# Start of a fused graph kernel: table and node constants move from VectorE to GpSimd, a shared PSUM tile, and a new order of rounds 0 to 3

## Chip, cores and metric

The kernel runs on one core of one Trainium2 chip. The metric is the device time of one execution in microseconds, as the median of several runs; less is better.

## What is computed

Two graph layers act on x, 3327 nodes of 64 features, with an adjacency matrix adj of 3327 x 3327 (about 0.5% ones). The part that costs time is all pairs of nodes (i, j): about 11 million of them.

```python
h = relu(layernorm(x))
# layer 0
x_t  = logmap0(h, c)                       # one scale per node
att  = sigmoid(left[:, None] + right[None, :] + b) * adj     # left = x_t @ w[:D], right = x_t @ w[D:]
x_local = logmap(h[:, None], h[None], c)   # per pair: a scale from dot products, times vectors of i and j
support = einsum('ij,ijd->id', att, x_local)
x = x + proj(expmap(h, support, c), c)
# layer 1
h = relu(layernorm(x)); s = h @ weight
rank = cumsum(adj != 0, axis=1)            # the last 100 neighbours get weights 0.5 ** (how many follow)
x = x + w @ s + bias
```

## The kernel before

**Tiling.** The nodes are padded to 26 blocks of 128. The pairs are cut into strips of target nodes i (8, 8, 6 and 4 blocks wide: `STRIPS`, L29), and each strip runs over all source blocks j from 25 down to 0. One *round* is one tile of 128 x up to 1024 pairs; in strip 0 a round is one block j, so round n handles j = 25 - n. There are 91 rounds.

**One round n**, by helper (lines of the kernel before):
- `load` (L613): SyncE's queue brings the adjacency tile `ad`; five buffers.
- `edges` (L620): VectorE makes the 0/1 `mask`. `count` (L625): TensorE adds the mask into the running count `pc` in PSUM. `read` (L638): the count is read out to `behind`; `ON_ACT` (L35) says on which engine, in strip 0 in turn VectorE (even rounds) and ScalarE (odd rounds).
- `products` (L668): TensorE multiplies the tables `ju` and `jz` (features of block j) with `iu`, `iz` (features of the strip) into a PSUM tile `pq`; there are two of these, used in turn. Two Gelus on ScalarE (L1211, L1212) turn `pq` into the pair's scale.
- `sigmoids` (L651): ScalarE's tanh of left + right into `sg`. `pair_one` (L658): VectorE, sg = (sg + 1) * ad. `pair_two` (L663): VectorE, sg = (pq + WD) * sg.
- `total` (L676): TensorE, `hw`-transposed times sg, summed over j in the PSUM tile `po`. `hw` is a summing table: 64 scaled features and one column for each node.

A strip's sum is then turned and finished per node (`post`, L978), in part on GpSimd; last come the second layer's products (L1252 on).

**The order of work** is written out by hand for TensorE, VectorE and ScalarE (`manual_schedule`, L692): each of the three runs its instructions in the order in which the program states them, and a wait holds up all that follows on that engine. GpSimd and SyncE are ordered by the scheduler. The loop at L1194 starts with round 1; in round n it also counts and reads round n + 1 and makes the mask of round n + 2.

**The start.** Ahead of the loop the features are normalised and scaled. Blocks 24-25 (`last_j`), 0-7 (`first_i`) and 16-23 (`high`) become tables before the loop: `features`, a cast, a subtraction (each feature is kept as two fp16 parts), transposes by TensorE (`turned_to`, L786), copies out of PSUM (`kept`, L794: VectorE `ju`, ScalarE `jz`), and `logits` (L855), which gives `left` and `right` of those blocks. Blocks 8-15 (`low`) are scaled at L896-899 and turned in `last_of_ahead` (L901), which the loop resumes once in each of rounds 1, 2 and 3 (L1238). There VectorE also makes `hw` (L907-911 and L915) and eleven small constants (L917-927). `left_to_dram` (L594) writes `left` out for the later strips. In PSUM `po` has one buffer, shared in turn by logits, `first_left`, the low blocks' transposes, `left_to_dram` and the strip's sum.

GpSimd starts with seven small loads (L460, L471-472), sets constants, and issues six copies of tables (L846).

Of the kernel before, what the change touches and what calls it, by code (L numbers as in the profile page):

```python
# [11 lines left out]
F32 = mybir.dt.float32  # L12
# [10 lines left out]
P = 128  # L23
# [9 lines left out]
AHEAD, LOADS = 1, 4  # L33
SGB, ADB = 5, 5
# [411 lines left out]
def fast(ctx, tc, x, adj_t, r, w_att, b_att, weight, bias, out, flag):  # L446
# [18 lines left out]
    bias_b = across(bias, D, "bias_b")  # L465

# [3 lines left out]
    for half in (slice(0, D), slice(D, P)):  # L470
        nc.gpsimd.dma_start(w_lr[half], bass.AP(tensor=w_att.tensor, offset=w_att.offset, ap=[[1, D], [D, 2]]))  # L471
        nc.gpsimd.dma_start(w2[half], weight)
# [121 lines left out]
    def left_to_dram():  # L594
        plt = ps.tile([P, P], F32, name="po")
# [42 lines left out]
    def read(n, j):  # L638
# [5 lines left out]
        if i * num // den != (i + 1) * num // den:  # L644
# [199 lines left out]
    for to, of in ((jz[:D], iz[D:]), (jz[D:], iz[:D]), (ju[:D], iu[:D]), (ju[D : D + 3], iu[D + 3 : D + 6]),  # L844
                   (ju[D + 3 : D + 6], iu[D : D + 3]), (ju[KB : KB + 7], iu[D:])):
        nc.gpsimd.dma_start(to[:, first_i], of)  # L846

# [7 lines left out]
    def logits(bs):  # L855

        plr = ps.tile([P, NB, 2], F32, name="po")
# [14 lines left out]
    for j in js(0):  # L872
        read(0, j)
    products(0)
    pl = first_left()
    turned_to(p3, high, 0)
    edges(1)
    pq = pq_of[0]
    A.activation(pq, pq, AF.Gelu, scale=-WG / QS)
    A.activation(pq, pq, AF.Gelu, scale=WH)  # L880
# [3 lines left out]
    pair_one(0)  # L884
    for j in js(1):
        count(1, j)
    products(1)
    edges(2)
    A.copy(left_b[:, : strips[0].F], pl[:, : strips[0].F])
    strips[0].left = left_b  # L890
    sigmoids(1)
    for j in js(1):
        read(1, j)
    pair_two(0)
    logits((high,))
    features(low)  # L896
    A.copy(nz[:, low, 0], zf[:, low])
    V.tensor_copy(nu[:, low, :D], zf[:, low])
    V.tensor_sub(nz[:, low, 1], zf[:, low], nz[:, low, 0])

    def last_of_ahead():  # L901

        p4 = ps.tile([P, 16, P], F16, name="po")
        turned_to(p4, low, 0)
        kept(p4, low, 0)
        wn, opx = small("wn"), small("opx")
        V.tensor_scalar(wn, nrm, WA / 2, None, op0=ALU.mult)  # L907
        V.tensor_scalar(opx, x2, c_c, 1.0, op0=ALU.mult, op1=ALU.add)
        V.tensor_mul(hw[:, :, D], opx, wn)
        V.tensor_mul(wn, wn, y)  # L910
        V.tensor_mul(hw[:, 13:, :D], rl[:, 13:], wide(wn[:, 13:], 13))
        logits((low,))
        left_to_dram()
        yield
        V.tensor_mul(hw[:, :13, :D], rl[:, :13], wide(wn[:, :13], 13))  # L915
        yield
        V.tensor_scalar(w2s, w2, 2.0**27 / HS, None, op0=ALU.mult)  # L917
        V.tensor_scalar(ih, babs, 2 / WA, None, op0=ALU.mult)
# [461 lines left out]
```

## Time and profile before

| what | value |
|---|---|
| median of 3 runs | 418.63 us (418.58 to 420.04) |
| the profiled execution | 419.95 us, of which 418.2 us are the span of the trace |
| VectorE (DVE) busy | 377.5 us, 90% of the span |
| ScalarE (ACT) busy | 362.8 us, 87% |
| TensorE (PE) busy | 359.9 us, 86% |
| GpSimd (POOL) busy | 113.4 us, 27%; idle from 27.7 us to 145 us but for one small copy |
| granted TensorE clock, mean | 0.973 |
| round 4's pair_one starts at | 53.42 us |
| a round pair of strip 0, later on | 6.87 us |

The page names source lines (L661 is line 661) and tiles: `sg<-sg,ad` is pair_one, `sg<-pq,sg` pair_two, `mask<-ad` edges, `behind_hi<-pc` a read. Busy shares are means over stages with different limits, so this case has to be read from the timeline between 20 and 60 us. There a start is in us from the span's beginning, then comes the duration, and in brackets the idle time before the instruction and what ended it. Instructions of one engine overlap by some 0.08 us, so the distance of starts is a better measure of cost than the duration.

### The profile page before, as it was taken

The page shows a single profiled execution, that of the slowest core. Times are in us where ns is not written, and L with a number is a line of the kernel's source. Part 1 is how long each engine was busy: PE and PEld are TensorE (multiplying, and loading weights), DVE is VectorE, ACT ScalarE, POOL GpSimd, SP SyncE. Part 2 cuts the span into 40 slices and gives each one's busy share as a digit, 9 for nine tenths or more (in the row PEclk, how much of TensorE's full clock was granted, in tenths as well). Part 3 has the DMA queues.
Part 4 walks back from the last instruction along what each step waited for, and adds up shares of the span by engine and source line. Part 5 has one row for each costly group of instructions (what it writes and reads, how often), then busy time and mean ns, then how long its engine had stood idle before and what let it go on. Part 6 is the DMA issues. An engine that isn't in the chain of part 4 may idle for free. (4 is left out here: it accounts for less than half of the span.)

```text
span 418.2 us, 4717 instructions
## 1 busy us (share of the span) xinstructions
PE 359.9 (86%) x1460; PEld 154.2 (37%) x1460; DVE 377.5 (90%) x559; ACT 362.8 (87%) x409; POOL 113.4 (27%) x224
## 2 busy tenths in 40 slices
PE   0094999999998899999999899999877999898792
PEld 0062333333333333333333444444332333344362
DVE  4989999999999999999999998899989899898841
ACT  3577889999999999999999999999896999787810
POOL 7020000000000073950250063801405183442400
PEclk9999799999999999999999999999898999999987
DMA  7313634444547445444535455444633420000012
GB/s 180 160 40 102 191 100 153 150 153 150 155 146 233 138 127 175 141 121 143 147 116 159 113 152 146 123 146 127 186 116 103 113 88 0 2 0 1 2 25 65
DMA packets 23298, 48.99 MB, mean 117 GB/s; under 512 B 8789, under 2 KB 9245, under 8 KB 23265
## 3 DMA queue, kind: packets, MB, share of 16 engines
q1 hardware_dynamic: 20993, 47.66, 37.9%
q0 software_dynamic: 464, 0.49, 0.7%
q10 hardware_dynamic: 1808, 0.46, 0.6%
q8 instruction: 13, 0.21, 0.2%
q14 instruction: 20, 0.16, 0.1%
HBM read 46.40 MB, written 0.87 MB: 113 GB/s over the span
## 5 line engine op out<-in xcount | busy, mean ns | idle before, releaser
L683 PE MATMUL po<-sg,hw 128*65 128x512 f32 (+1 forms) x364 | 162.2, 570 | 0.4 <-DVE st L958 0.4
L666 DVE SCALAR_TENSOR_TENSOR sg<-pq,sg 128x1024 f32<-128x1024 f32 (+1 forms) x91 | 103.5, 1137 | 7.4 <-ACT pq L1212 6.8
L661 DVE SCALAR_TENSOR_TENSOR sg<-sg,ad 128x1024 f32<-128x1024 f32 (+1 forms) x91 | 103.8, 1140 | 0.1
L656 ACT ACTIVATE sg<-left_b,right 128x1024 f32<-128x1024 f32 (+2 forms) x103 | 99.5, 978 | 0.0
L1211 ACT ACTIVATE pq<-pq 128x1024 f32<-128x1024 f32 (+1 forms) x90 | 86.1, 957 | 2.7 <-PE pq L674 2.5
L1212 ACT ACTIVATE pq<-pq 128x1024 f32<-128x1024 f32 (+1 forms) x90 | 85.2, 946 | 2.9
L683 PEld LDWEIGHTS po<-sg,hw 128*65 128x65 f32 x364 | 49.7, 139 | 70.8 <-issue 56.9
L634 PE MATMUL pc<-mask,ca 128*128 128x512 bf16 (+1 forms) x175 | 64.3, 368 | 12.4 <-DVE behind_hi L649 3.8
L673 PE MATMUL pq<-iu,ju 71*128 71x512 f16 (+1 forms) x182 | 67.8, 373 | 1.5 <-ACT jz L797 1.0
L635 PE MATMUL pc<-mask,cb 128*128 128x512 bf16 (+1 forms) x182 | 65.5, 370 | 1.8 <-ACT behind_lo L645 1.7
L674 PE MATMUL pq<-iz,jz 128*128 128x512 f16 (+1 forms) x182 | 66.3, 371 | 0.0
L623 DVE TENSOR_SCALAR mask<-ad 128x1024 bf16<-128x1024 f32 (+1 forms) x91 | 58.7, 645 | 0.0
L1280 PE MATMUL pw<-wt,s 128*128 128x512 bf16 (+1 forms) x154 | 34.2, 376 | 4.2 <-DVE s L1135 2.2
L635 PEld LDWEIGHTS <-cb 128*128 128x128 bf16 x182 | 17.9, 98 | 53.2 <-issue 41.5
L1030 POOL TENSOR_TENSOR dots<-dots,ih 128x8 f32<-128x8 f32 (+1 forms) x3 | 2.2, 720 | 129.0 <-DVE dots L1050 129.0
L634 PEld LDWEIGHTS <-ca 128*128 128x128 bf16 x175 | 17.3, 99 | 29.6 <-issue 17.7
L1280 PEld LDWEIGHTS <-s 128*128 128x128 f16 x182 | 18.0, 101 | 23.8 <-issue 4.3
L673 PEld LDWEIGHTS <-ju 71*128 71x128 f16 x182 | 18.0, 99 | 22.8 <-DVE sg L666 4.3
L674 PEld LDWEIGHTS <-jz 128*128 128x128 f16 x182 | 18.1, 100 | 19.5 <-issue 2.3
L645 ACT ACTIVATE behind_lo<-pc 128x1024 uint8<-128x1024 f32 (+2 forms) x29 | 24.9, 858 | 0.0
L645 ACT ACTIVATE behind_hi<-pc 128x1024 uint8<-128x1024 f32 (+2 forms) x23 | 19.7, 858 | 5.6 <-PE pc L635 5.6
L1285 POOL TENSOR_TENSOR x_sb<-x_sb,bias_b 128x256 f32<-128x256 f32 (+1 forms) x6 | 9.9, 1657 | 51.0 <-DVE w L1119 45.5
(317 smaller groups left out, 366.8 us busy)
## 6 DMA issues: line engine op xcount, KB each, us to landing
ad<-in_adj_t SPq DMA_DIRECT2D x65, 512.0 KB, 3.6
ad<-in_adj_t SPq DMA_DIRECT2D x26, 384.0 KB, 3.2
out<-o SPq DMA_DIRECT2D x6, 128.0 KB, 1.9
left_b<-left_d SPq DMA_DIRECT2D x1, 512.0 KB, 4.0
x_sb<-in_x ACTq DMA_DIRECT2D x1, 416.0 KB, 5.6
x_sb<-in_x SPq DMA_DIRECT2D x1, 416.0 KB
left_b<-left_d SPq DMA_DIRECT2D x1, 384.0 KB
jz<-iz POOLq DMA_DIRECT2D x2, 128.0 KB, 2.6
```

Source lines behind the costliest of these rows:

```text
L623: V.tensor_scalar(*args, 0.0, None, op0=ALU.not_equal)
L634: T.matmul(S.pc[:, f0:f1], ca, S.before[:, f0:f1], start=False, stop=True, skip_group_check=True)
L635: T.matmul(S.pc[:, f0:f1], cb, now[:, f0:f1], start=S.first, stop=True, skip_group_check=True)
L656: A.activation(part(n, sg, j), S.left[:, : S.F], AF.Tanh, bias=right[:, j : j + 1], scale=0.5)
L661: V.scalar_tensor_tensor(sg, sg, 1.0, ad_of.pop(n)[:, :w], op0=ALU.add, op1=ALU.mult)
L666: V.scalar_tensor_tensor(sg, pq_of.pop(n)[:, :w], WD, sg, op0=ALU.add, op1=ALU.mult)
L673: T.matmul(part(n, pq, j, f0, f1), ju[:KB, j, :], S.iu[:, f0:f1], start=True, stop=False)
L674: T.matmul(part(n, pq, j, f0, f1), jz[:, j, :], S.iz[:, f0:f1], start=False, stop=True)
L683: T.matmul(S.po[: D + 1, f0:f1], hw[:, j, :], part(n, sg_of[n], j, f0, f1), start=j == NB - 1, stop=j == 0)
L1211: A.activation(pq, pq, AF.Gelu, scale=-WG / QS)
L1212: A.activation(pq, pq, AF.Gelu, scale=WH)
L1280: T.matmul(pw[n], s2[:, j].rearrange("p c d -> p (c d)"), wt[:, f0:f1].bitcast(BF16), start=j == order[0], stop=j == NB - 1)
```

## The change

- **GpSimd takes** the 64 feature columns of `hw` (seven multiplications of at most 4 blocks, highest blocks first) and nine of the eleven constants. VectorE keeps the column hw[:, :, D], `wn`, `opx`, `balm` and the reciprocal `sk`. The loads of `bias_b` and `w2` move in the source behind the table copies on GpSimd's queue (as built, they stand behind its constants and before the table copies, and the multiplications stand behind the table copies).
- **Low blocks**: they are scaled before round 1's mask, and turned through a tile of the `pq` ring (p5), whose PSUM space the low logits and the transposed `left` then use too. `po` is free for the sum of round 0 earlier.
- **Reads** of rounds 0 and 2 go from VectorE to ScalarE.
- **Order**: rounds 0 and 1 are finished, and round 0 is summed, ahead of the loop, which now starts with round 2; masks, counts and reads of rounds 2 and 3 have new places, and `total(1)` comes in round 2. From round 4 on the order is as it was.

```diff
@@ -31,6 +31,7 @@
 JD = range(12, 16)
 IN_ORDER = {mybir.EngineType.PE, mybir.EngineType.DVE, mybir.EngineType.Activation}
 AHEAD, LOADS = 1, 4
+EARLY = 3
 SGB, ADB = 5, 5
 ON_ACT = ((1, 2), (5, 8), (3, 4), (1, 2))
 
@@ -462,14 +463,11 @@
 
     r_c = across(r, 1, "r_c")
     batt = across(b_att, 1, "batt")
-    bias_b = across(bias, D, "bias_b")
-
     w_lr = const.tile([P, 2], F32, name="w_lr")
     w2 = const.tile([P, D], F32, name="w2")
     w2s = const.tile([P, D], F32, name="w2s")
     for half in (slice(0, D), slice(D, P)):
         nc.gpsimd.dma_start(w_lr[half], bass.AP(tensor=w_att.tensor, offset=w_att.offset, ap=[[1, D], [D, 2]]))
-        nc.gpsimd.dma_start(w2[half], weight)
 
 
     def column(value, name):
@@ -591,8 +589,7 @@
             T.transpose(pl[:, b * P : (b + 1) * P], left[:, b : b + 1].to_broadcast([P, P]), ident)
         return pl
 
-    def left_to_dram():
-        plt = ps.tile([P, P], F32, name="po")
+    def left_to_dram(plt):
         T.transpose(plt[:NB, :], left, ident)
         V.tensor_copy(left_t, plt[:NB, :])
         nc.sync.dma_start(left_d.rearrange("(b p) -> b p", p=P), left_t)
@@ -635,13 +632,13 @@
             T.matmul(S.pc[:, f0:f1], cb, now[:, f0:f1], start=S.first, stop=True, skip_group_check=True)
         S.before, S.first = now, False
 
-    def read(n, j):
+    def read(n, j, on_act=None):
         k, lo, hi = rounds[n]
         S = strips[k]
         kept = behind(j)[:, S.i0 : S.i0 + S.F]
         num, den = ON_ACT[k]
         i = NB - 1 - j
-        if i * num // den != (i + 1) * num // den:
+        if on_act or (on_act is None and i * num // den != (i + 1) * num // den):
             A.activation(kept, S.pc[:, : S.F], AF.Relu, scale=128.0 if j in JD else 1.0)
         elif j in JD:
             V.tensor_scalar(kept, S.pc[:, : S.F], 0.0, 128.0, op0=ALU.max, op1=ALU.mult)
@@ -844,6 +841,9 @@
     for to, of in ((jz[:D], iz[D:]), (jz[D:], iz[:D]), (ju[:D], iu[:D]), (ju[D : D + 3], iu[D + 3 : D + 6]),
                    (ju[D + 3 : D + 6], iu[D : D + 3]), (ju[KB : KB + 7], iu[D:])):
         nc.gpsimd.dma_start(to[:, first_i], of)
+    bias_b = across(bias, D, "bias_b")
+    for half in (slice(0, D), slice(D, P)):
+        nc.gpsimd.dma_start(w2[half], weight)
 
     V.tensor_mul(yr, yr, g[:, :NB])
     V.scalar_tensor_tensor(yr, yr, f_c, babs, op0=ALU.mult, op1=ALU.mult)
@@ -852,9 +852,15 @@
     A.copy(nz[:, high, 0], zf[:, high])
     V.tensor_copy(nu[:, high, :D], zf[:, high])
 
-    def logits(bs):
-
-        plr = ps.tile([P, NB, 2], F32, name="po")
+    def gelus(n):
+        pq = pq_of[n][:, : span(n)]
+        A.activation(pq, pq, AF.Gelu, scale=-WG / QS)
+        A.activation(pq, pq, AF.Gelu, scale=WH)
+
+    def logits(bs, plr=None):
+
+        if plr is None:
+            plr = ps.tile([P, NB, 2], F32, name="po")
         for p in bs:
             for b in range(p.start, p.stop):
                 z = iz[:, b, :] if p is first_i else jz[:, b, :]
@@ -870,61 +876,69 @@
     logits((first_i, last_j))
     V.tensor_sub(nz[:, high, 1], zf[:, high], nz[:, high, 0])
     for j in js(0):
-        read(0, j)
+        read(0, j, True)
     products(0)
     pl = first_left()
     turned_to(p3, high, 0)
+    features(low)
+    V.tensor_copy(nu[:, low, :D], zf[:, low])
+    wn, opx = small("wn"), small("opx")
+    V.tensor_scalar(wn, nrm, WA / 2, None, op0=ALU.mult)
+    V.tensor_scalar(opx, x2, c_c, 1.0, op0=ALU.mult, op1=ALU.add)
+    V.tensor_mul(hw[:, :, D], opx, wn)
+    V.tensor_mul(wn, wn, y)
+    for b in (24, 20, 16, 12, 8, 4, 0):
+        n = min(4, NB - b)
+        G.tensor_mul(hw[:, b : b + n, :D], rl[:, b : b + n], wide(wn[:, b : b + n], n))
     edges(1)
-    pq = pq_of[0]
-    A.activation(pq, pq, AF.Gelu, scale=-WG / QS)
-    A.activation(pq, pq, AF.Gelu, scale=WH)
+    gelus(0)
     strips[0].left, left_b = pl, strips[0].left
     sigmoids(0)
     kept(p3, high, 0)
     pair_one(0)
+    A.copy(nz[:, low, 0], zf[:, low])
+    pair_two(0)
     for j in js(1):
         count(1, j)
     products(1)
-    edges(2)
     A.copy(left_b[:, : strips[0].F], pl[:, : strips[0].F])
     strips[0].left = left_b
+    V.tensor_sub(nz[:, low, 1], zf[:, low], nz[:, low, 0])
     sigmoids(1)
+    gelus(1)
+    logits((high,))
+    pair_one(1)
+    p5 = ps.tile([P, FMAX], F32, name="pq", bufs=2)
+    p4 = p5.bitcast(F16).rearrange("p (b q) -> p b q", q=P)
+    turned_to(p4, low, 0)
+    kept(p4, low, 0)
     for j in js(1):
-        read(1, j)
-    pair_two(0)
-    logits((high,))
-    features(low)
-    A.copy(nz[:, low, 0], zf[:, low])
-    V.tensor_copy(nu[:, low, :D], zf[:, low])
-    V.tensor_sub(nz[:, low, 1], zf[:, low], nz[:, low, 0])
+        read(1, j, True)
+    pair_two(1)
+    total(0)
+    logits((low,), p5[:, : 2 * NB].rearrange("p (b c) -> p b c", c=2))
+    left_to_dram(p5[:, FMAX - P :])
+    edges(2)
+    products(2)
+    sigmoids(2)
+    for j in js(2):
+        count(2, j)
+    edges(3)
 
     def last_of_ahead():
 
-        p4 = ps.tile([P, 16, P], F16, name="po")
-        turned_to(p4, low, 0)
-        kept(p4, low, 0)
-        wn, opx = small("wn"), small("opx")
-        V.tensor_scalar(wn, nrm, WA / 2, None, op0=ALU.mult)
-        V.tensor_scalar(opx, x2, c_c, 1.0, op0=ALU.mult, op1=ALU.add)
-        V.tensor_mul(hw[:, :, D], opx, wn)
-        V.tensor_mul(wn, wn, y)
-        V.tensor_mul(hw[:, 13:, :D], rl[:, 13:], wide(wn[:, 13:], 13))
-        logits((low,))
-        left_to_dram()
+        V.tensor_scalar(balm, bal, MIN_NORM, None, op0=ALU.max)
+        V.reciprocal(sk, balm)
         yield
-        V.tensor_mul(hw[:, :13, :D], rl[:, :13], wide(wn[:, :13], 13))
-        yield
-        V.tensor_scalar(w2s, w2, 2.0**27 / HS, None, op0=ALU.mult)
-        V.tensor_scalar(ih, babs, 2 / WA, None, op0=ALU.mult)
-        V.tensor_scalar(balm, bal, MIN_NORM, None, op0=ALU.max)
-        V.tensor_mul(su, nrm, balm)
-        V.tensor_mul(sv, bal, su)
-        V.reciprocal(sk, balm)
-        V.tensor_scalar(sk, sk, sqc, None, op0=ALU.mult)
-        V.tensor_scalar(maxnorm, absr, 1.0 - EPS_BALL, None, op0=ALU.mult)
-        V.tensor_mul(c2_c, c_c, c_c)
-        V.tensor_scalar(m2c, c_c, -2.0, None, op0=ALU.mult)
-        V.tensor_scalar(p2c, c_c, 2.0, None, op0=ALU.mult)
+        G.tensor_scalar(w2s, w2, 2.0**27 / HS, None, op0=ALU.mult)
+        G.tensor_scalar(ih, babs, 2 / WA, None, op0=ALU.mult)
+        G.tensor_mul(su, nrm, balm)
+        G.tensor_mul(sv, bal, su)
+        G.tensor_scalar(sk, sk, sqc, None, op0=ALU.mult)
+        G.tensor_scalar(maxnorm, absr, 1.0 - EPS_BALL, None, op0=ALU.mult)
+        G.tensor_mul(c2_c, c_c, c_c)
+        G.tensor_scalar(m2c, c_c, -2.0, None, op0=ALU.mult)
+        G.tensor_scalar(p2c, c_c, 2.0, None, op0=ALU.mult)
         ahead.close()
 
         behind_of["lo"] = ctx.enter_context(tc.tile_pool(name="lo", bufs=1, side="right", reuse_waits="tile")).tile(
@@ -1191,7 +1205,8 @@
     stages, rest_of_ahead = [Stage(range_steps())], last_of_ahead()
     range_end = in_range()
     load(LOADS)
-    for n in range(1, R):
+    load(LOADS + 1)
+    for n in range(2, R):
         k, lo, hi = rounds[n]
         m, w = n + AHEAD, span(n)
         ended, turned = (n > i and rounds[n - i - 1][1] == 0 for i in (1, 2))
@@ -1199,7 +1214,8 @@
             if rounds[n + LOADS][2] == NB:
                 strip_in(rounds[n + LOADS][0])
             load(n + LOADS)
-        two = m < R and len(js(m)) == 2
+        fresh = EARLY <= m < R
+        two = fresh and len(js(m)) == 2
         if two:
             count(m, js(m)[0])
         early = n >= 4 and not turned
@@ -1207,28 +1223,31 @@
             pa = turn(k - 1)
         elif early:
             total(n - 2)
-        pq = pq_of[n][:, :w]
-        A.activation(pq, pq, AF.Gelu, scale=-WG / QS)
-        A.activation(pq, pq, AF.Gelu, scale=WH)
+        gelus(n)
         asked_of_act()
         if turned:
             finish()
             stages.append(Stage(per_node(k - 1, pa)))
         pair_one(n)
-        if m + 1 < R:
+        if EARLY <= m + 1 < R:
             edges(m + 1)
+        if n == 2:
+            for j in js(2):
+                read(2, j, True)
+        if n < 4:
+            products(n + 1)
         if two:
             read(m, js(m)[0])
-        if m < R:
+        if fresh:
             count(m, js(m)[-1])
         if n + 1 < R:
             sigmoids(n + 1)
-        if m < R:
+        if fresh:
             read(m, js(m)[-1])
-        if n + 1 < R:
+        if 4 <= n < R - 1:
             products(n + 1)
-        if n > 1 and not turned and not early:
-            total(n - 2)
+        if n == 2:
+            total(1)
         if ended:
             strip_out(k - 1)
         if hi - lo > 1:
```

## The prediction

> **What bounds the kernel now.** First the slices of the page, then three stretches of the trace, then VectorE's timeline in the second of them.
>
> ```profile
> DVE  4989999999999999999999998899989899898841
> ACT  3577889999999999999999999999896999787810
> ```
> ```profile
> 30.26:53.42 23.16, 16.14 (x93) 7.26 (x92) 21.78 (x44) 18.45 (x19) 0.19 (x1) 0.85 0.43 132
> 61.00:130.00 69.00, 69.00 (x241) 26.41 (x239) 68.93 (x75) 68.36 (x71) 0.00 (x0) 1.00 0.51 155
> ```
>
> A row of the second view gives the busy time of TensorE, its weight loads, VectorE, ScalarE and GpSimd, then TensorE's clock. From 61 us on VectorE is busy 68.93 of 69 us: nothing is late there, so what a round costs is fixed, and only the moment at which this state is reached can move. In 30.26 to 53.42 VectorE is busy 21.78 of 23.16 us (1.38 idle), ScalarE only 18.45, GpSimd 0.19. VectorE sets the end of this stretch, and part of what it does there is not a round's work:
>
> ```profile
> 34.14 0.68 DVE L784 TENSOR_TENSOR sq<-rl,yz 128x512 f32<-128x512 f32 x1
> 34.85 0.43 DVE L898 CAST nu<-sq 128x512 f16<-128x512 f32 x1
> ...
> 37.88 1.22 DVE L649 TENSOR_SCALAR behind_hi<-pc 128x1024 uint8<-128x1024 f32 x1
> ...
> 41.55 1.03 DVE L911 TENSOR_TENSOR hw<-rl,wn 128x832 f32<-128x832 f32 x1
> ...
> 46.42 1.00 DVE L915 TENSOR_TENSOR hw<-rl,wn 128x832 f32<-128x832 f32 x1
> ...
> 53.42 1.22 DVE L661 SCALAR_TENSOR_TENSOR sg<-sg,ad 128x1024 f32<-128x1024 f32 x1
> ```
>
> The last row is round 4's pair_one, from which on both kernels have one order. I ask when it starts after the change. The other engines wait for the low blocks' tables:
>
> ```profile
> 40.86 1.01 ACT L797 COPY jz<-po 128x1024 f16<-128x1024 f16 x1 [2.35 <-DVE ju L796]
> ```
> ```profile
> 41.93 0.59 PE L862 MATMUL po<-w_h,jz 128*128 128x2 f16 x16 [4.09 <-ACT jz L797]
> ```
>
> ScalarE stood 2.35 us until VectorE had copied `ju`, and TensorE 4.09 us behind both.
>
> **What the Trainium skill says.** (1) "SBUF — State Buffer", section "Who interferes with whom": a VectorE instruction with two SBUF inputs contends with a GpSimd instruction that reads SBUF, and the later one waits for the whole of the other. The trace agrees in one place only: beside GpSimd's bias addition (L1285) this pair_one took 1.31 us, two rounds earlier 0.95:
>
> ```profile
> 293.26 1.31 DVE L661 SCALAR_TENSOR_TENSOR sg<-sg,ad 128x768 f32<-128x768 f32 x1
> ```
>
> The pair_one at 356.10 us, started beside such an addition, took its usual 1.20. (2) "GPSIMD Engine Reference", section "3.1 Elementwise — side-by-side cycle accounting": a two-input operation takes about 2.6 cycles an element, nearly twice VectorE's time. Here it is dearer, and I use the trace: 128x256 took 1.57 us on average (0.72 to 2.31), VectorE's 128x512 0.60 from start to start. (3) "TensorE: Matmul & The Clock Gate", section "What's actually happening": after an idle window of some 3.4 us the array runs at half clock, until a busy one; the windows run freely. The trace agrees: behind the idle 4.09 us matmuls of 512 columns stand 0.43 us apart, from 48.6 us on 0.22.
>
> **The change, step by step.** Unchanged up to 26.6 us: the start is bound by the arrival of x (VectorE waits 6.0 us) and a chain of small steps. Moving three loads (0.55 us of issue each) behind GpSimd's constants makes these 1.6 us earlier; nobody waits for them, so zero. The loads themselves (8.9 us to landing) hold GpSimd's queue at `w2s` to perhaps 17 us; behind it stand other constants and the six table copies, which cannot start before 24.5 us anyway. Zero; cover 7 us.
>
> *VectorE, 26.6 to 30.3 us.* Removed: round 0's read (1.13 from start to start). Added: low features, cast and the `wn` group (0.70 + 0.43 + 0.80). Now 26.6 + 0.6 + 1.9 + 0.6 (mask) = 29.7. In both kernels `ju` of the high blocks waits for TensorE's transposes, to 30.26. So 1.9 us moves into an idle stretch free of charge (there were 1.26 us idle, and the read's 1.13). ScalarE does the read at 26.0 (0.9); the Gelus and tanh of round 0 then end at 30.0, before pair_one(0) needs them at 30.87.
>
> *VectorE, 30.26 to pair_one(4).* Removed from the 21.78 us: two `hw` multiplications 1.00 + 0.94; low features and cast 1.13; `wn` group 0.80; round 2's read 1.14; nine constants 0.91 (51.96 to 53.42 is 1.46 for eleven, 0.55 of it for the two kept). Sum 5.92; left 15.86. The masks, pairs, logits and copies are the same in number. If the idle time stayed at 1.38, pair_one(4) would start at 47.5. It doesn't: VectorE has become quick enough to wait for the others. Walking through with durations from start to start (Gelu pair 1.97, tanh 1.04, read 0.9, `jz` copy 0.9, four matmuls 0.87, `total` 1.72):
> - pair_two(0) ends at 33.1, low subtraction at 33.7. ScalarE: `jz` 30.98 to 31.9, cast to 32.4, `left_b` to 33.35, tanh(1) to 34.4, Gelus(1) to 36.4. High logits need `po` from `left_b`: TensorE 33.4, VectorE 34.2 to 34.65. Idle 0.46.
> - pair_one(1) to 35.8, `ju` low (transposed 33.95 to 35.2) to 36.4, pair_two(1) to 37.6. ScalarE's `jz` low 36.5 to 37.4, 4.5 us earlier than at present.
> - Low logits and the transposed `left` go now ahead of products(2) on TensorE, which runs in order. From the end of `jz` it took 0.68 us to VectorE's `left`, 1.48 to `left_t`: 38.1 and 38.9; VectorE idle 0.8. This is the added wait: behind it stand products(2), hence Gelus(2). products(2) 38.5 to 39.5; ScalarE has read(1) and tanh(2) in the meantime, to 39.3, so it loses 0.4. `total(0)` (35.2 to 36.9) lies before, in the time in which `jz` is made.
> - Two masks to 40.4, pair_one(2) 41.55, mask, pair_two(2) 42.15 to 43.3, two constants to 43.85, pair_one(3) to 45.0, mask to 45.6. ScalarE: Gelus(2) to 41.7, read(2) 42.6, tanh(3) 43.7, read(3) 44.6, Gelus(3) 46.5, tanh(4) 47.6.
> - read(4) is VectorE's and needs count(4), which stands behind `total(1)` (43.5 to 45.2) and products(4): ready at 47.1. Idle 1.5. Then read and pair_two(3): pair_one(4) at **49.3**, against 53.42.
>
> Check by the other sum: 15.86 busy and 0.46 + 0.8 + 1.5 + some 0.2 = 3.0 idle give 49.1. Gain 4.1 us. Rounds 5 and 6, walked on, keep it (pair_one(6) at 56.9, not 60.96), and ScalarE is further ahead than that (Gelus(4) at 47.6, not 55.7), so the two reads that it took over (1.8 us) cost nothing.
>
> *GpSimd's multiplications.* They start when `wn` is there, 29.5 (the copies' issue ends at 27.7), and take six times 1.57 and a half: to about 40. `total(0)` needs the first alone (30.3 against 35.2), total(2) the second (32 against 47). Hidden, cover 5 us. What they cost VectorE by contention: nothing, as at 356 us, up to 0.36 for each of the four pair_ones and subtractions in that time, 1.4 us. I take 0.4. Below nothing there is no mechanism.
>
> *Loads.* load(6) follows pair_one(1) (35.8, not 37.3), load(7) pair_one(2); each keeps two rounds against 3.6 us to landing. Zero.
>
> Sum: 4.1 - 0.4 = 3.7 us. The profiled execution was 419.95 us (span 418.2 and 1.75 around it), so 416.25; taken from the median 418.63: **414.9**.
>
> **Rivals.**
> (A) The walk holds: 414.9, by bounds of contention and of the idle 1.5 between 413.6 and 416.3.
> (B) TensorE falls to half clock. The tiny logits and transposes between 33 and 35 us, or the pause at 41.2 to 42.6, make a window slack. For: at present it happens at 40 us, and PEclk is 0.66 in 40 to 50. Against: the 4.09 us wait that brought it about is gone; my longest pause is 1.4. A cold `total(0)` or `total(1)` costs 1.7 and matmul groups 0.87 each; 1.3 to 3 arrive at VectorE, I take 2.2: 417.1.
> (C) Given back later. At the turns of the strips the clock is halved twice (300 to 303, 317 to 320 us), and VectorE idles 0.96, 0.44, 1.00 and 0.94 around it. The windows fall differently in a schedule that is moved by 4 us; one more such pair takes back 3.3: 418.2.
> (D) Slower: GpSimd holds VectorE. From 29.5 to 42 VectorE has about six instructions on two SBUF tensors or masks. If each waited for a whole multiplication, 6 x 1.57 = 9.4, of which some 1.4 of idle hides: 8.0 - 4.1 = 3.9 too much, 422.5. It decides from 4.1 us of unhidden waiting. Against: the largest hold in the trace is 0.36.
> That the change doesn't do as it says I exclude: the built order shows the reads and multiplications on their new engines.
>
> **How the numbers follow.** A 0.63, B 0.19, C 0.11, D 0.07. About 0.5% (2.1 us: below 416.5, above 420.7) is what a measurement of this kernel can tell from no change. Faster: all but a sliver of A (0.62) and the better part of B's low end (0.08), 0.70; slower: D, 0.07; same: the rest, 0.23. The range leaves out C's worse half, D and A's best end: 413.6 to 418.2.
>
> **What would show it.** Right: pair_one of round 4 between 48.5 and 50.5 us; round 0's pair_one still near 30.9; ScalarE's wait before `jz` low gone; VectorE's largest idle time ahead of read(4), released by TensorE; 6.87 us for two rounds after it. Wrong: matmuls 0.43 us apart between 34 and 48 (B); pair_ones over 1.5 us beside the multiplications (D); pair_one(4) early and the end not (C); or VectorE waiting for a Gelu in rounds 2 to 6, which would mean that ScalarE, with the reads, has become the bound.

## The result, and the profile after

The changed kernel took 416.26 us, the median of 7 runs (415.32 to 418.25). The kernel before, run beside it, took 419.53 (418.22 to 420.16). The ratio is 0.9935, with a 95% interval from 0.9909 to 0.996: faster by 0.65%, 0.4 to 0.9. The forecast was 414.9 in a range of 413.6 to 418.2. It was 1.36 us too low. About 0.9 us of this is the base: 418.63 in the runs shown, 419.53 now. The other 0.46 is gain that was not there: 3.73 forecast, 3.27 between the medians.

The profiled execution of the changed kernel happens to be the slowest of its seven (418.25 us, span 416.4). So it shows a gain of 1.70 us against the profiled execution of before (419.95), about half of what the medians show. That is luck, and it shows where time can be lost again. First, the slices of the page after; each digit is a fortieth of the span, some 10.4 us:

```profile
DVE  4999799999999899999999798899989899898841
ACT  3589999999998899999999899999996999788810
PEclk9998999999999899999999899999898999999987
```

The fourth slice of PEclk, 31 to 42 us, has an 8, as half clock in the start (rival B) would give it. The slices that begin at 135 and 229 us have an 8 too, and beside them VectorE falls to 8 and to 7. Before the change VectorE showed a run of nines there. Next, rows by stretch (busy time of TensorE, weight loads, VectorE, ScalarE, GpSimd, then TensorE's clock):

```profile
30.26:50.00 19.74, 16.85 (x97) 7.21 (x97) 16.88 (x25) 19.04 (x20) 7.70 (x9) 0.91 0.52 155
61.00:130.00 69.00, 68.25 (x233) 25.83 (x236) 68.97 (x74) 67.89 (x70) 0.00 (x0) 1.00 0.55 162
130.00:140.00 10.00, 7.44 (x25) 2.86 (x25) 9.39 (x12) 8.67 (x12) 0.00 (x0) 0.83 0.41 113
```

In the first stretch ScalarE is now busy 19.04 of 19.74 us and VectorE 16.88. VectorE is idle for 2.86 us, where it had 1.38 in the longer stretch up to 53.42 us before. The plateau from 61 us on is as before: VectorE busy 68.97 of 69. The third stretch, behind the first turn of a strip, has a clock of 0.83; before the change it was 1.00. VectorE's timeline between 32 and 50 us shows the steps of the walk:

```profile
32.53 0.99 DVE L906 TENSOR_TENSOR d<-sq,d 128x512 f16<-128x512 f32 x1
...
37.51 0.17 DVE L870 TENSOR_TENSOR left<-pq,yr 128x8 f32<-128x8 f32 x1 [0.42 <-PE pq L868]
...
46.83 1.22 DVE L646 TENSOR_SCALAR behind_hi<-pc 128x1024 uint8<-128x1024 f32 x1 [1.95 <-PE pc L632]
...
49.10 1.21 DVE L658 SCALAR_TENSOR_TENSOR sg<-sg,ad 128x1024 f32<-128x1024 f32 x1
```

The last row is pair_one of round 4: 49.10, where the walk put it at 49.3 and the kernel before had it at 53.42. The largest idle time of this stretch is the predicted one, ahead of the read of round 4 and released by TensorE. ScalarE's `jz` copy of the low blocks, TensorE's first matmuls behind it and GpSimd's multiplications are now, in one row each from the timelines of these engines:

```profile
35.78 1.01 ACT L794 COPY jz<-pq 128x1024 f16<-128x1024 f16 x1
```
```profile
36.85 0.55 PE L868 MATMUL pq<-w_h,jz 128*128 128x2 f16 x16 [0.91 <-ACT jz L794]
```
```profile
28.90 6.72 POOL L892 TENSOR_TENSOR hw<-rl,wn 128x128 f32<-128x128 f32 x7 [1.42 <-DVE wn L889]
```

ScalarE's wait of 2.35 us is gone (no bracket), TensorE's 4.09 us have become 0.91, and seven multiplications ended at 35.6, not at 40.

**Where the time went.** I compare the start of pair_one in each round, before minus after, and call it the gain. It was 0.72 us in round 0, 2.21 in round 1, 4.03 in round 2, 4.32 in rounds 3 and 4. It then stood still to within 0.01 us through round 30. By round 31 it was 2.64, from round 50 on 3.02, after round 55 some 1.4, and it was 1.45 in round 90. So the change gave what it should by 49 us. Two losses of about 1.67 us, each behind the turn of a strip, then took it down; some 0.4 us came back after the first and 0.1 after the second, so that two thirds of the gain were gone at the end. This is the first turn on TensorE after the change:

```profile
133.04 0.71 PE L1165 MATMUL po<-ident,sg 65*128 65x65 f32 x8 [2.51 <-ACT sg L1159]
...
135.11 0.63 PE L670 MATMUL pq<-iu,ju 71*128 71x512 f16 x1
135.54 0.63 PE L671 MATMUL pq<-iz,jz 128*128 128x512 f16 x1
135.97 4.64 PE L680 MATMUL po<-sg,hw 128*65 128x512 f32 x8
```

TensorE waits 2.51 us until the sums have been copied out (L1159), then transposes them. From 134.7 us matmuls of 512 columns stand 0.43 us apart instead of 0.22, and the total takes 4.64 us. The same place before the change:

```profile
137.36 0.71 PE L1151 MATMUL po<-ident,sg 65*128 65x65 f32 x8 [2.50 <-ACT sg L1145]
...
138.77 0.38 PE L673 MATMUL pq<-iu,ju 71*128 71x512 f16 x1
138.99 0.38 PE L674 MATMUL pq<-iz,jz 128*128 128x512 f16 x1
...
139.64 3.61 PE L683 MATMUL po<-sg,hw 128*65 128x512 f32 x8
```

The pause is as long (2.50), but nothing slows down behind it. At the second turn the pause is 1.50 us in both kernels. The clock's records show what differs. All half-clock stretches in them, but for the last of a trace, which the end of the program cuts off, last 3.41 us or a multiple of it, and within a trace they lie multiples of 3.41 us apart. So each trace has a grid of windows. The next rows give, after the change and before it, the window of this grid with most of the pause in it and the window behind; TensorE's busy time stands behind the length:

```profile
131.23:134.64 3.41, 1.54 (x12) 1.03 (x14) 3.07 (x5) 2.20 (x3) 0.00 (x0) 1.00 0.41 141
134.64:138.06 3.42, 3.42 (x7) 1.23 (x6) 3.42 (x5) 3.42 (x6) 0.00 (x0) 0.50 0.48 123
```
```profile
135.89:139.31 3.42, 1.95 (x15) 1.23 (x16) 3.08 (x5) 2.56 (x4) 0.00 (x0) 1.00 0.31 110
139.31:142.72 3.41, 3.41 (x11) 1.08 (x9) 3.41 (x5) 3.41 (x5) 0.00 (x0) 1.00 0.47 149
```

After the change 1.8 of the 2.5 us fell into one window, in which TensorE was busy for 45%, and the next is at half clock. Before, two windows shared the pause, the emptier one was busy for 57%, and the next is at full clock. VectorE paid for the difference in a later round, where no such wait stood before:

```profile
145.03 1.22 DVE L646 TENSOR_SCALAR behind_hi<-pc 128x1024 uint8<-128x1024 f32 x1 [1.78 <-PE pc L632]
```

### The profile page after: what moved, and what is told of

It is laid out like the page before. It is cut to its first block, busy times and chain, and to the rows that moved or that the text cites. A ratio compares the mean times of both kernels' runs of the same rounds, so it can differ in the third digit from the quotient of the medians.

```text
span 416.4 us, 4699 instructions
## 1 busy us (share of the span) xinstructions
PE 361.1 (87%) x1436; PEld 154.4 (37%) x1460; DVE 373.1 (90%) x546; ACT 364.8 (88%) x411; POOL 124.0 (30%) x240
## 4 chain that ended last, share of the span: by engine, by line
DVE 33%; ACT 27%; PE 24%; issue 10%; POOL 3%; DMA 1%; DVEq 0%; POOLq 0%; ACTq 0%
DVE sg L663 9%; PE po L680 9%; ACT sg L653 8%; DVE sg L658 8%; ACT pq L857 8%; ACT pq L858 3%; DVE wt L1287 3%; PE pq L670 3%; PE pq L671 3%; DVE behind_lo L646 3%; PE pc L632 2%; PE pc L631 2%; ACT behind_lo L642 2%; ACT behind_hi L642 2%; PE pw L1299 2%
## 5 line engine op out<-in xcount | busy, mean ns | idle before, releaser
L680 PE MATMUL po<-sg,hw 128*65 128x512 f32 (+1 forms) x364 | 164.5, 576 | 0.5 <-DVE st L972 0.4
L857 ACT ACTIVATE pq<-pq 128x1024 f32<-128x1024 f32 (+1 forms) x91 | 87.1, 957 | 3.5 <-PE pq L671 3.2
L858 ACT ACTIVATE pq<-pq 128x1024 f32<-128x1024 f32 (+1 forms) x91 | 86.2, 947 | 2.9
L631 PE MATMUL pc<-mask,ca 128*128 128x512 bf16 (+1 forms) x170 | 62.1, 365 | 11.1 <-DVE behind_hi L646 3.9
L671 PE MATMUL pq<-iz,jz 128*128 128x512 f16 (+1 forms) x182 | 67.2, 376 | 0.0
L632 PE MATMUL pc<-mask,cb 128*128 128x512 bf16 (+1 forms) x168 | 60.1, 368 | 2.2 <-ACT behind_lo L642 1.7
L642 ACT ACTIVATE behind_hi<-pc 128x1024 uint8<-128x1024 f32 (+2 forms) x25 | 21.8, 872 | 5.3 <-remote 3.3
```

The lines of the kernel that those rows point to most:

```text
L631: T.matmul(S.pc[:, f0:f1], ca, S.before[:, f0:f1], start=False, stop=True, skip_group_check=True)
L632: T.matmul(S.pc[:, f0:f1], cb, now[:, f0:f1], start=S.first, stop=True, skip_group_check=True)
L642: A.activation(kept, S.pc[:, : S.F], AF.Relu, scale=128.0 if j in JD else 1.0)
L671: T.matmul(part(n, pq, j, f0, f1), jz[:, j, :], S.iz[:, f0:f1], start=False, stop=True)
L680: T.matmul(S.po[: D + 1, f0:f1], hw[:, j, :], part(n, sg_of[n], j, f0, f1), start=j == NB - 1, stop=j == 0)
```

## Experiments

Two theories. T1: what is gained by round 4 is work taken off VectorE less the new waits; it then stays, and only half-clock windows that open behind TensorE's pause at a turn take back some 1.7 us each, by chance. T2: the turn gives it back whatever the clock does, because ScalarE, with two reads more, has no slack there. Gains are read as above, each from one profiled execution against that of before. The start alone differs between executions of the same code: round 0's gain is 0.09 and 0.33 us in two kernels that are the kernel before up to 130 us, and 0.11 to 0.95 us in six that are the kernel after through round 1. Where it matters I therefore also give the growth of the gain from round 0 to round 4, which is 3.60, 3.63 and 3.62 us in three executions of the changed order. Medians and ratios are against runs of the kernel before on the same chip (medians 419.69, 419.56, 419.46).

**1. No pause at the turns.** TensorE repeats the products of the round twice ahead of the transposes; the same values are written again, so this is added work alone.

```diff
         if turned:
+            for _ in range(2):
+                again(n)      # products(n) into the same tile
             pa = turn(k - 1)
```

In the kernel before:

> The kernel before; at each turn of a strip TensorE repeats the round's products twice in the time in which it waits for the copy of the sum (same result, extra work only). Theory 1 (what the change gains by round 4 stays, but a half-clock window of TensorE after this pause takes some 1.7 us back, by chance): the clock stays full at all turns, pair_one of round 4 stays at 53.4 us, and the time falls from 419.5 to 418.0 to 418.8. Theory 2 (the turns are limited by ScalarE or the order of work, whatever the clock): no faster than before, or up to 1 us slower by the extra work.

It took 421.1 us (22 runs), ratio 1.0028 [1.0011, 1.0044]: slower, where T1 had expected 418.0 to 418.8. The gain stayed within 0.02 us of nothing through rounds 4 to 76 and fell to -3.0 behind the third turn: -1.74 in round 80, the rest with a half-clock stretch of 6.8 us from 316.8 us on, where the kernel before had one of 3.4. At this turn the added work lay on the path, and the pause lay behind the transposes and not ahead of them. TensorE's rows at the third turn of this kernel:

```profile
312.52 0.38 PE L680 MATMUL pq<-iu,ju 71*128 71x512 f16 x1
...
314.26 0.53 PE L1158 MATMUL po<-ident,sg 65*128 65x65 f32 x6
317.65 0.58 PE L634 MATMUL pc<-mask,ca 128*128 128x512 bf16 x1 [2.85 <-DVE behind_hi L649]
```

Before, the transposes stood at 312.52; the filling put them at 314.26, and the pause of 2.85 us came as before. The same edit in the kernel after:

> The changed kernel with the same filling of TensorE's pause at each turn. Theory 1: the two drops of 1.67 us at rounds 30 and 55 are gone, pair_one of round 90 is 4.0 to 4.4 us ahead of the kernel before with its pause filled, the time is 414.0 to 415.0. Theory 2: the drops remain, 416 to 417.5.

It took 416.14 us (8 runs), ratio 0.9926 [0.9894, 0.9957]. In its profile no stretch between 25 and 393 us is at half clock, and the gain stands at 4.07 from round 4 (4.06 in round 76): both losses are gone, as T1 says. But the median is no better than without the filling, and lies in T2's range and not in T1's 414.0 to 415.0. The edit was too wide: at the third turn the gain falls by 1.7 us again (4.82 in round 79, 3.07 in round 80). In this execution, with no half clock at that turn either, it was back at 4.76 by round 90, so the profile doesn't show what the other runs lost.

**2. Filled at the first two turns only** (`2 if k < 3 else 0` in place of 2).

> The kernel before with TensorE's pause filled by repeated products at the turns behind strips 0 and 1 only; at the third turn the pause lies behind the transposes, and the filling stood in their way there. Both theories: the kernel before showed no half-clock window at these two turns in its profile, so the modal time stays, 418.5 to 420; only its slow tail gets shorter.

419.22 us (22 runs), ratio 0.9981 [0.9965, 0.9996]; gain 0.46 in round 4, 0.38 in round 90.

> The changed kernel with the same two pauses filled. Theory 1 (a half-clock window behind the pause takes the gain back, by chance): no drop at rounds 30 and 55, the gain of round 4 (4.0 to 4.4 us) is still there at round 76, the median is 414.8 to 415.8, and the difference to the kernel before so filled is 3.7 to 4.5 us. Theory 2 (the turn itself gives it back): the difference stays at 3.3 or less.

415.21 us (5 runs, 414.75 to 416.24), ratio 0.9894 [0.9872, 0.9916]. The gain is 4.44 in rounds 4 to 31 and 4.40 in round 57. Its stretch behind the first turn, and TensorE there:

```profile
130.00:140.00 10.00, 9.18 (x40) 3.75 (x40) 9.39 (x12) 8.66 (x11) 0.00 (x0) 1.00 0.41 112
```
```profile
132.92 0.71 PE L1172 MATMUL po<-ident,sg 65*128 65x65 f32 x8 [0.76 <-ACT sg L1166]
...
134.33 0.38 PE L670 MATMUL pq<-iu,ju 71*128 71x512 f16 x1
134.55 0.38 PE L671 MATMUL pq<-iz,jz 128*128 128x512 f16 x1
```

The pause is 0.76 us instead of 2.51, the clock 1.00 instead of 0.83, and matmuls stand 0.22 us apart. With both kernels so filled, the change is worth 419.22 - 415.21 = 4.01 us by the medians and 3.6 by the two ratios. T1 expected 3.7 to 4.5, T2 at most 3.3. The ratios' intervals, some 1.1 us wide to each side taken together, don't exclude T2 by themselves; the profiles do, since in them ScalarE and VectorE have the same work at the turn and lose nothing. Nor does it take the filling: over all the kernels of this study, a lasting loss of 1.3 to 2.7 us at rounds 30 and 55 is found in every profile with half clock behind that turn, and in no other. Two kernels of the changed order, unfilled and with ScalarE's two reads (experiments 4 and 7), had no half clock at either turn and lost nothing (gains of 1.65 and 1.92 us in round 20, 1.64 and 1.88 in round 90); that of experiment 5 had it at the first turn alone, and lost 1.65 us there and nothing at the second.

**3. The added wait before the read of round 4.** `total(1)` is moved from ahead of products and count of round 4 to behind them.

```diff
-        if n == 2:
-            total(1)
...
         if 4 <= n < R - 1:
             products(n + 1)
+        if n == 3:
+            total(1)
```

> The changed kernel with total(1) moved behind count(4) and products(4) on TensorE, so that VectorE's read of round 4 no longer waits for it. If this wait of 1.95 us is VectorE's last slack ahead of the steady state, pair_one of round 4 moves from 49.1 to 47.3 to 47.7 us, and half to all of it stays: 414.5 to 415.6. If TensorE is as near its limit as VectorE, the wait comes back at read(6): pair_one of round 8 gains under 0.5, 416.2.

415.59 us (6 runs), ratio 0.9905 [0.9871, 0.994], not to be told from the change by the medians. Its profiled execution had half clock behind both turns and ended at 419.84. Up to there it shows what the edit does. VectorE's waits ahead of the reads of rounds 4 and 6:

```profile
45.84 1.22 DVE L646 TENSOR_SCALAR behind_hi<-pc 128x1024 uint8<-128x1024 f32 x1 [0.41 <-PE pc L632]
...
53.59 1.22 DVE L646 TENSOR_SCALAR behind_hi<-pc 128x1024 uint8<-128x1024 f32 x1 [0.49 <-ACT pq L858]
```

The wait of 1.95 us became 0.41, and the gain in round 4 rose from 4.32 to 5.31, although this execution had begun 0.54 us later (0.18 in round 0). From round 0 to 4 the gain grew by 5.1 us instead of 3.6. Half a microsecond came back as a wait two rounds later (released through ScalarE's Gelu), so 4.73 stood from round 6. The step "added wait" is shown: of the 1.95 us, `total(1)` caused 1.5, of which about 1.0 could be kept by another order.

**4. The multiplications back on VectorE**, at the same place, in two blocks of 13.

```diff
-    for b in (24, 20, 16, 12, 8, 4, 0):
-        n = min(4, NB - b)
-        G.tensor_mul(hw[:, b : b + n, :D], ...)
+    for b in (13, 0):
+        n = 13
+        V.tensor_mul(hw[:, b : b + n, :D], ...)
```

> The changed kernel with the summing table's 64 columns multiplied by VectorE again (two of 128x832), at the same place behind the low features. No slack stands behind this place but 0.2 us, so theory 1 expects all of 1.9 us on round 0's pair_one (32.0 for 30.15) and on ScalarE's jz copy behind it; at round 4 1.5 to 1.9 us (50.6 to 51.0), time 417.8 to 418.5. The rival (VectorE has 3 us of idle in this stretch, which swallow it) expects under 0.5 us at round 4, 416.3.

418.27 us (20 runs), ratio 0.9976 [0.9962, 0.999]. VectorE's rows:

```profile
29.34 1.96 DVE L892 TENSOR_TENSOR hw<-rl,wn 128x832 f32<-128x832 f32 x2
...
34.81 0.68 DVE L906 TENSOR_TENSOR d<-sq,d 128x512 f16<-128x512 f32 x1
```

The gain in round 4 is 1.65 and stays so to round 90, since no half-clock window opened at its turns. That is 4.32 - 1.65 = 2.7 us less, but 0.5 us of it was there before the edit (the copy L836 began at 23.80 us, in the kernel after at 23.30). The part costs about 2.2 us, some more than the 1.96 us that the multiplications take and than the 1.5 to 1.9 expected. TensorE was at half clock from 31.8 to 38.6 us here, and the low logits waited 0.91 us; whether that comes of the edit is not shown. So this part alone is worth about half of the change. The subtraction of L906, which took 0.99 us beside GpSimd, takes 0.68 without it.

**5. Each of GpSimd's multiplications done twice**, with the same result, to try the contention of rival D.

```diff
+        for _ in range(2):
             G.tensor_mul(hw[:, b : b + n, :D], ...)
```

> The changed kernel with each of GpSimd's seven multiplications made twice (the same values). My reading of the contention (0.3 to 0.5 us in all, single instructions on two SBUF tensors): they end near 42 for 35.6 us, nobody waits for them, and the gain at round 4 falls from 4.3 by 0.2 to 0.6; time within 0.6 us of the changed kernel. Rival (GpSimd holds VectorE for whole multiplications): 1.5 us or more lost at round 4.

417.13 us (20 runs), ratio 0.9941 [0.9921, 0.9961], not to be told from the change's 0.9935. GpSimd, and VectorE's pair_one of round 2 beside it:

```profile
28.89 11.40 POOL L893 TENSOR_TENSOR hw<-rl,wn 128x128 f32<-128x128 f32 x14 [1.42 <-DVE wn L889]
```
```profile
39.75 1.63 DVE L658 SCALAR_TENSOR_TENSOR sg<-sg,ad 128x1024 f32<-128x1024 f32 x1
```

That pair_one took 1.63 us instead of 1.21, the one of round 0 1.40, two masks 1.72 instead of 1.27. The wait ahead of the read of round 4 shrank from 1.95 to 1.12 us and took this up: the gain in round 4 is 4.77, and grew from round 0 on by 3.8. A fall by 0.2 to 0.6 had been expected. Doubling GpSimd's work costs nothing there. D, by which one set of multiplications was to hold VectorE for 9.4 us, is refuted.

**6. The two reads back on VectorE** (`read(0, j)` and `read(2, j)` without the engine's flag).

> The changed kernel with the reads of rounds 0 and 2 on VectorE again. Theory 1: 1.1 us on round 0's pair_one, as no slack stands there, and 0.5 to 1.2 more by way of count(3) and the read of round 4, so the gain at round 4 falls from 4.3 to 2.0 to 2.7 us, 417.5 to 418.5. Rival (VectorE's idle 1.95 us ahead of the read of round 4 swallow the second one, and ScalarE's earlier start gives some of the first back): gain 3.2 to 3.8, 416.5 to 417.3.

419.52 us (12 runs), ratio 1.0 [0.9974, 1.0025]. By its profile the reads are worth less than that. The gain is -0.20 in round 0 and 3.11 in round 4, so they cost 1.2 us there, not their 2.3 us of work. The first costs 0.9; the second is mostly swallowed by the wait ahead of the read of round 4, 1.35 us here. T1 had asked for a gain of 2.0 to 2.7; 3.11 lies nearer the rival's 3.2 to 3.8. Half clock behind both turns then took it to 0.14. The profiled run (419.49 us) lies at the median of its runs, and 1.24 above that of the change, which lost at both turns too. But the change's is the slowest of its seven, and so the medians are 3.3 us apart. The mean clock of the runs (mostly 0.965 to 0.977, against 0.969 to 0.983 after the change) says that half clock was more frequent here; why, the runs don't show.

**7. The low features, logits and left row through `po`**, as before; `total(0)`, which needs `po`, goes behind the counts of round 2.

```diff
-    p5 = ps.tile([P, FMAX], F32, name="pq", bufs=2)
+    p5 = ps.tile([P, FMAX], F32, name="po")
...
-    total(0)
...
     for j in js(2):
         count(2, j)
+    total(0)
```

> The changed kernel with the low blocks, their logits and the turned left in the single po buffer again, so that total(0) cannot come before them and stands behind count(2). Theory 1: the low tables lose 0.2 to 0.8 us; total(0)'s 1.72 us move into the line ahead of count(4): the gain at round 4 falls from 4.3 to 2.2 to 2.8, 417.3 to 418.2. Rival (po was not what held it up; TensorE has room): gain 3.8 to 4.3, 416.3.

418.35 us (12 runs), ratio 1.0007 [0.9975, 1.0039]; three of the runs took over 422.6, which puts the ratio above 1 though the median is low. The gain in round 4 is 1.93 (2.2 to 2.8 expected), 2.4 us less than with the change; VectorE waited 0.54 us for the transposes of the low tables, and the wait ahead of the read grew:

```profile
49.22 1.23 DVE L646 TENSOR_SCALAR behind_hi<-pc 128x1024 uint8<-128x1024 f32 x1 [2.78 <-PE pc L632]
```

The tile and the place of `total(0)` hang together, so this prices both: without them a good half of the gain is lost. TensorE was at half clock from 31.8 to 42.0 us in this execution, and part of the price may be that.

**8. GpSimd's part without the new order**: in the kernel before, the multiplications in seven blocks and the nine constants go to GpSimd.

> The kernel before, and of the change one part alone: the summing table's 64 columns and the nine constants on GpSimd, all else where it was. 2.85 us of work leave VectorE. Theory 1 (what is removed counts only where VectorE is not then waiting): the read of round 4 at 49.7 us waits for count(4) on TensorE, which runs in half clock behind the pause at 38 to 42 us, so the 1.94 us of multiplications turn into waiting, and only the 0.9 us of constants behind it move pair_one of round 4: gain there 0.8 to 1.3 us, 418.4 to 418.9. Rival (work removed is time gained): 2.5 to 2.9 us, 416.8.

419.63 us (14 runs), ratio 1.0013 [0.9994, 1.0032]: no gain. Its profiled execution began 1.38 us early (round 0), ahead of all that the edit moves on TensorE and VectorE: TensorE had left half clock earlier, so the transposes of the high blocks took less time and `ju` behind them no longer waited. The first half of these transposes, before and here:

```profile
28.32 1.06 PE L792 MATMUL pq<-id,nu 128*78 128x128 f16 x8
```
```profile
27.43 0.61 PE L792 MATMUL pq<-id,nu 128*78 128x128 f16 x8
```

In round 4 the gain was 2.52 and from round 6 1.5. Less the early start, 1.1 us of it is due to the edit in round 4, as T1 had said, and 0.1 from round 6 on, which the 418.4 to 418.9 expected had not foreseen. In the old order `wn` comes late, and so do the multiplications:

```profile
40.23 5.26 POOL L913 TENSOR_TENSOR hw<-rl,wn 128x128 f32<-128x128 f32 x7 [12.56 <-DVE wn L910]
```

VectorE, rid of 2.85 us of work, waited instead: 1.03 us ahead of the low logits, 0.88 ahead of the read of round 4 and 0.94 ahead of the next. Taking this work off VectorE is worth next to nothing as long as the tables that it waits for are not made earlier.

**9. Both repairs together**: edits 2 and 3 on the kernel after.

> The changed kernel with total(1) behind count(4) and with the pauses at the first two turns filled. Theory 1: the 0.9 us that total(1) late gained at equal start stay to the end when no half-clock window takes them: gain at round 6 and at round 76 4.9 to 5.4 us, median 414.2 to 415.0. If total(1) late gave its gain back anyway: 415.2, as with filling alone.

414.26 us (6 runs, 412.64 to 414.83), ratio 0.9867 [0.9835, 0.99]. It beats both kernels: its slowest run is faster than the fastest of the change. The gain is 5.90 in round 4, 5.33 from round 6, and still 5.25 in round 90. From 130 to 140 us, behind the first turn, its clock was 1.00.

**10. The transposed `left` later**, behind the counts of round 2, on top of that.

```diff
-    left_to_dram(p5[:, FMAX - P :])
     edges(2)
     products(2)
     sigmoids(2)
     for j in js(2):
         count(2, j)
+    left_to_dram(p5[:, FMAX - P :])
```

> As the kernel before it, and the turning of left for the later strips moved from ahead of products(2) to behind count(2). This takes out the wait that I named as added by the change: ScalarE's Gelus of round 2 start 0.2 to 0.5 us earlier, VectorE's idle 0.8 us around the low logits fall to 0.5. 0.1 to 0.5 us at round 4 if the read of round 4 follows, 413.9 to 414.9; nothing if the read then waits for TensorE.

414.58 us (6 runs, 411.62 to 415.81), ratio 0.987 [0.9831, 0.9909]: the same. From round 0 to round 4 the gain grew by 4.99 us, in the kernel without this edit by 4.94. The wait for the transposed row moved (1.01 us at its new place), and nothing was won.

## Why the prediction was right, and where it was off

- *"VectorE, 26.6 to 30.3"* was right in its cost: the low features and the `wn` group lie between 26.98 and 28.82 us and delay nothing. But `ju` of the high blocks, which was to wait for TensorE until 30.26 in both kernels, came at 29.54 without a wait, and pair_one(0) started at 30.15 instead of 30.87. Of that 0.72, which nobody had forecast, 0.24 had been there since the high features (24.48, not 24.72), which the change doesn't touch. The other 0.48 came because TensorE left half clock earlier: its clock record has the first full stretch from 28.83 us, before from 30.08. In the six executions of the changed order whose code is the same through round 1 this moment lies anywhere between 24.3 and 29.8 us, so the 0.72 is luck.
- *"VectorE, 30.26 to pair_one(4)"*: 49.3 us forecast, 49.10 measured. Two errors cancel in this. From pair_one(0) on the gain grew by 3.60 us and not by 4.1, and the early start made up for it. The idle time was right: 2.86 us between `ju` and pair_one(4), for 3.0. The busy time was not: 16.70 for 15.86. The sum takes 5.92 us, distances of starts with the small gaps in them, from a busy time; the removed instructions cover 5.34 us of it, and 16.43 are left. The rest, some 0.3, is about what GpSimd's contention added. The sum's 3.7 us, with contention in them, are close to what came. Experiment 4 shows the largest single piece. Experiment 8 shows why the sum may not be read as work removed alone: there 2.85 us removed gave at most 1.1.
- *"Added wait"*, 0.8 us ahead of the low logits and `left`: 0.42 measured, and TensorE's pause 0.91. The idle time ahead of the read of round 4, put at 1.5, was 1.95; experiment 3 confirms that `total(1)` stands before it.
- *GpSimd's multiplications* were over-priced: 6.72 us for 6.5 blocks, about 1.0 each, where a row of another operation (L1285) had given 1.57. Their contention was put at 0.4 (0 to 1.4); the longer rows sum to about 0.4 (the subtraction 0.31 of it, a small addition behind it 0.08), and experiment 5 shows that the wait behind them covers even twice the multiplications. "SBUF — State Buffer", section "Who interferes with whom", of the Trainium skill says that the two engines contend for a pair of ports under "an exclusive lock", by which the later instruction would wait for the rest of the other. Here instructions beside multiplications of 1 us became longer by 0.1 to 0.4 us or not at all, so the measurement decides against the full price.
- *Rival B*, TensorE at half clock in the start, came in part: matmuls stood 0.43 us apart from 39.1 to 42.5 us. It cost at most some 0.2 us, not the 2.2 it was given: the profiles of experiments 1 and 2, whose code is the same up to there, have full clock in this place, and their wait ahead of the read of round 4 is 1.73 instead of 1.95. As A and B weren't exclusive, a chance for each was the wrong form.
- *Rival C*, given back later, is what happened in the profiled execution: 2 x 1.67 us, the size it had (3.3), of which some 0.5 came back. It had a chance of 0.11, as an event that either comes or doesn't. In fact half clock is drawn anew in each run: the mean clock of the seven runs lies between 0.969 and 0.983, and one window of 3.41 us at half clock is worth 0.004 of that (3.41 x 0.5 / 416, an estimate), so they differ by three or four such windows, at the turns or elsewhere. The term of the sum that was off is its last, in which the gain at round 4 was carried to the end without a price: 3.73 instead of 3.27 us between medians, while with the turns filled the same change was worth 4.01.
- *Windows at the turns.* "TensorE: Matmul & The Clock Gate", section "What's actually happening", of the Trainium skill says that windows run freely, and the traces agree: pauses of 2.50 and 2.51 us had different outcomes, and the grid of 3.41 us lies elsewhere in each trace. How busy TensorE was in the emptiest window at the first turn goes with the outcome in all eight profiles without filling: at 26 to 45% half clock followed (four profiles), at 52 to 62% full clock (four). At the second turn, where the pause is 1.50 us, it is less clear: 56% was followed by half clock in three profiles and by full clock in two, 62 to 66% by full clock in three. So the place of the window decides at the first turn as far as these profiles go; where the limit lies they don't show.
- *Rival D* is refuted by experiment 5, *loads* cost nothing (`w2s` held GpSimd till 14.41 us, ten before it was next needed).
- The base: 418.63 was the median of three runs, 0.9 us under the next median. This is two thirds of the miss and no error of the walk.

What stays open: whether the change makes the half-clock windows at the turns likelier, or only moved. The kernel before has none in its one profile; but the filling of two turns made it faster by 0.2 to 1.5 us (0.9981 [0.9965, 0.9996]), so it too may have had some in runs that were not profiled. In both kernels the pause at the first turn is equally long. If the grid of windows could lie anywhere with equal chance, the emptiest window there would be less than half busy in 73% of the cases before and 75% after; this is an estimate from TensorE's busy time in the two profiles, and it gives the change no reason to make such windows likelier, but no run shows it. Of the parts of the change, the nine constants and the new order of rounds 0 and 1 were not tried alone.

## What to carry to other kernels

When an engine that sets the pace is relieved, walk the other engines through the same stretch: here 5.3 us of busy time removed became 3.6 us of gain from round 0 to round 4, and 2.85 us removed without the new order became 0.1. Compare more than one profile of the same code: the start alone was worth 0.7 us of the gain here, and that was chance. Then follow the gain round by round to the end, since it can be given back at a place which the change doesn't touch. Where TensorE pauses ahead of work on the path, give it something to do, but only where the pause lies ahead of that work; at the third turn the same filling cost 1.7 us and more.

## What the hardware showed that was not expected

- A pause of 2.5 us on TensorE, in the same place and of the same length, was followed by half clock in some executions and not in others, and so was one of 1.5 us; half clock cost 1.3 to 2.7 us at a turn. One kernel's runs spread over 3 us (415.32 to 418.25), and this is a likely part of it.
- GpSimd's two-input multiplication of 128x256 took 0.8 to 1.0 us (6.72 us for 6.5, 11.40 for 13, 5.26 for 6.5 in experiment 8), although another addition of 128x256 in the same kernel averaged 1.57. VectorE's work of the same size beside it grew by at most 0.4 us.
- The same code starts its first round up to 0.8 us earlier or later from execution to execution (gains of 0.11 to 0.95 in round 0). Much of it goes with the moment at which TensorE leaves half clock, which lay between 23.9 and 30.1 us over all profiles. A comparison of two profiles must take this off before it prices an edit of half a microsecond.
